# A state-space layer with a small mixture of experts: LayerNorm statistics on ScalarE, the experts' relus on VectorE, a router without its division

## The chip, the cores and the metric

The kernel runs on one core of a Trainium2 chip. The metric is the device time of one execution in microseconds (us). The core has five engines that run side by side, each from its own queue in order: TensorE (PE in the profile, with its weight loads as PEld), VectorE (DVE), ScalarE (ACT), GpSimd (POOL) and SyncE (SP), which only issues DMAs here. A difference of 0.5% (about 10 us) is about what a measurement of this kernel can tell from no change.

## The reference

The input `u` has 4 sequences of 2048 rows of 256 numbers. The layer is

```python
x = x + ssm(layernorm(x), ...)        # selective state space, 512 channels, 16 states each
x = x + moe(layernorm(x), ...)        # 4 experts, the best 2 of them per row

# ssm, per step of the sequence
dA = exp(dt_t[..., None] * A);  dB = dt_t[..., None] * Bt[:, None, :]
h = h * dA + x_t[..., None] * dB
y_t = einsum('bdn,bn->bd', h, Ct)

# moe
scores = softmax(x @ Wg.T + bg);  topv, topi = top_k(scores, 2)
w = sum(one_hot(topi) * topv)
h = relu((x @ Wi.T)[:, None, :] + lora)      # lora: a rank-4 term of each expert
out = einsum('bse,bsed->bsd', w, h @ Wo.T)
```

All numbers are fp32. The hidden width of the experts is 1024. The base product `x @ Wi.T` and the output product with `Wo` are shared by the experts; only the rank-4 term differs.

## The kernel before

The rows are cut into 16 chunks of 512 (`NCHUNK`), four per sequence. Sizes that matter: `P` = 128 partitions, `NJ` = 4 blocks of 128 rows in a chunk, `DM` = 256, `E` = 4 experts.

**The loop.** Each chunk has 64 "states": four blocks of 128 channels times 16 states. Line 996 loops over all 1024 states. For a state, `decay` (line 858) lets ScalarE compute `dA = exp(a * delta)` for 512 time steps, `enter` (line 863) lets GpSimd compute the inputs `dBx` of two states at once, `scan` (line 875) lets VectorE run the recurrence, `read` (line 888) multiplies the result by `C` (on VectorE, tile `hC`; for 5 states in 16 on GpSimd, tile `hP`), and `sum_y` (line 902) lets PE add it up, transposed, in PSUM (tile `y`). `keep` copies the last column to `carry` on ScalarE. ScalarE writes the `dA` of a state two states ahead of the scan (`AHEAD_A`), and GpSimd's `dBx` is four ahead (`AHEAD_B`).

**Work around the loop.** For each chunk there is a front (LayerNorm of the next chunk, `layernorm_T` with the names `ua`, `xn_a`; the input products `pin`; `delta` with a softplus; `xdt`; a gate `g` with a silu), and, after the chunk's last scan, a tail (`po`, the output product) and the experts (`ffn`, line 587): LayerNorm (`xn_f`, `x2T`), router (`plg`), and then eight pieces k = 0..7 (4 blocks of 128 rows times the 2 halves of the hidden width). For each k, `p_low` and `p_base` make the pre-activation `pz` in one PSUM bank, a relu makes `h`, `p_hT` transposes it (`phT`), `a_hT` copies it to `hT`, and `p_down` makes the output `pf`, which `add` adds to `u`.

**Statistics.** `stats` (line 334) runs `bn_stats` and `bn_aggr` on VectorE for each of the 4 blocks; `rstd` (line 341) is four small GpSimd instructions; `norm` applies scale and bias on ScalarE.

**Two experts in one bank.** A row's second expert (slot 1) is computed first: its rank-4 term and the base are added up in the bank and ScalarE takes `relu(topv1 * z)`. Then PE adds the difference of the two rank-4 terms to the same bank and ScalarE takes `relu(topv0 * z)` (`a_relu`, line 734, two calls for each k). `p_hT` adds the two by transposing both into one PSUM bank. In the last chunk alone (`late`) it goes another way: `ratio` (line 721) divides the second weight by the first, ScalarE takes the first relu with that ratio, `d_relu` (line 729) on VectorE takes `max(z, 0) + h`, only one tile is transposed, and `add` multiplies by the first weight.

**The order.** The order of instructions on each engine is decided by a planner when the program is built (`Pacer`, line 45). It carries a planned clock for each engine, and each piece of work is a `Step` with an engine, a cost in us and the steps that it comes after. The loop's own steps are written in order; `fill` (line 107) places waiting steps between them as long as they are planned to start and end close to VectorE's planned time. A VectorE step is placed only if what it waits for on other engines is planned to end 0.7 us earlier (`LATENCY` plus `MARGIN`). `begin` (line 926) hands the threads of steps to the planner; the next chunk's first four `stats` steps are made ready by the softplus of the chunk before:

```python
stats = norms[c + 2][:NJ]
stats[0].after = [loaded, st[c + 1]["soft"]]
```

Once the last scan is written, `drain` writes what is left. PSUM has three banks (`BANKS`) for all work around the loop.

Of the kernel before, what the change touches and what calls it, by code (L numbers as in the profile page):

```python
# [8 lines left out]
F32 = mybir.dt.float32  # L9
AF = mybir.ActivationFunctionType  # L10
ALU = mybir.AluOpType
# [161 lines left out]
def ssm_moe_layer_kernel(  # L173
# [40 lines left out]
    NCHUNK = B * CPB  # L214
    SHARED = (0, 3, 6, 9, 12)
# [114 lines left out]
    def layernorm_T(src, dst, name, then=None):  # L330
# [3 lines left out]
        def stats(j):  # L334
            if j == 0:
                q["mv"] = small.tile([P, NJ, 2], F32, tag=f"mv{name[0]}", name=f"mv_{name}")
            x = small.tile([P, 6], F32, tag="st", name=f"st_{name}_{j}")
            dve.bn_stats(x, src()[:, j, :])
            dve.bn_aggr(q["mv"][:, j, :], x)

        def rstd():

            ve = small.tile([P, NJ], F32, tag="ve", name=f"ve_{name}")
            q["rstd"] = small.tile([P, NJ], F32, tag="rstd", name=f"rstd_{name}")
            q["nmr"] = small.tile([P, NJ], F32, tag="nmr", name=f"nmr_{name}")
            pool.tensor_scalar_add(ve, q["mv"][:, :, 1], EPS)
            pool.tensor_tensor(q["rstd"], ve, mhalf, ALU.pow)
            pool.tensor_tensor(ve, q["mv"][:, :, 0], q["rstd"], ALU.mult)
            pool.tensor_scalar_mul(q["nmr"], ve, -1.0)

        def norm(j):
            q["xn", j] = work.tile([P, DM], F32, tag=f"xn{j}", name=f"xn_{name}_{j}", bufs=1)
            act.activation(
                q["xn", j], src()[:, j, :], AF.Identity,
# [15 lines left out]
        steps = [Step("dve", 0.54, lambda j=j: stats(j)) for j in range(NJ)]  # L370
        steps += [Step("pool", 1.95, rstd)]
# [215 lines left out]
    def ffn(c):  # L587
# [31 lines left out]
        def exp_():  # L619
            for j in range(NJ):  # L620
                act.activation(room(1)[:, j, :], room(0)[:, j, :], AF.Exp, bias=q["red"][:, j : j + 1])

        def softmax():
            sm = small.tile([P, NJ], F32, tag="sm", name=f"sm_{c}")
            dve.tensor_reduce(sm, room(1), AX.X, ALU.add)
            dve.reciprocal(sm, sm)
            p_ = q["p"] = small.tile([P, NJ, E], F32, tag="p_", name=f"p_{c}")
            dve.tensor_tensor(p_, room(1), sm[:, :, None].to_broadcast([P, NJ, E]), ALU.mult)
            dve.tensor_copy(room(2), p_)
# [4 lines left out]
            p_j = room(2)[:, :, None, :].to_broadcast([P, NJ, E, E])  # L634
            p_i = p_[:, :, :, None].to_broadcast([P, NJ, E, E])
            dve.tensor_tensor(eq, p_j, p_i, ALU.is_equal)
            dve.tensor_tensor(gt, p_j, p_i, ALU.is_gt)
            dve.tensor_tensor(eq, eq, lower[:, None, :, :].to_broadcast([P, NJ, E, E]), ALU.mult)
            dve.tensor_tensor(eq, eq, gt, ALU.add)
            dve.tensor_reduce(room(1), eq, AX.X, ALU.add)  # L640

            m = q["m"] = small.tile([P, TOPK, NJ, E], F32, tag="m", name=f"m_{c}")
            for k in range(TOPK):
                dve.tensor_scalar(m[:, k], room(1), float(k), None, ALU.is_equal)
# [12 lines left out]
        def top():  # L657

            m = q["m"]
            mp = small.tile([P, TOPK, NJ, E], F32, tag="mp", name=f"mp_{c}")  # L660
            pool.tensor_tensor(mp, m, q["p"][:, None, :, :].to_broadcast([P, TOPK, NJ, E]), ALU.mult)
            s["topv"] = fold(mp, (P, TOPK, NJ), "topv").rearrange("p k j o -> p k (j o)")
# [58 lines left out]
        def ratio():  # L721

            s["top0"] = small.tile([P, NJ], F32, tag="top0", name=f"top0_{c}", bufs=1)
            dve.tensor_copy(s["top0"], s["topv"][:, 0, :])
            r = small.tile([P, NJ], F32, tag="sm", name=f"r_{c}")
            dve.reciprocal(r, s["top0"])
            dve.tensor_tensor(s["topv"][:, 1, :], s["topv"][:, 1, :], r, ALU.mult)

        def d_relu(k):

            q["h", k, 0] = q["h", k, 1]
            dve.scalar_tensor_tensor(q["h", k, 1], q["z", k], 0.0, q["h", k, 1], ALU.max, ALU.add)

        def a_relu(k, slot):

            h = q["h", k, slot] = scanp.tile([P, HF], F32, tag="hC", name=f"h{slot}_{c}_{k}", bufs=4) if late else work.tile([P, HF], F32, tag=f"h{slot}", name=f"h{slot}_{c}_{k}")
            act.activation(h, q["z", k], AF.Relu, scale=s["topv"][:, slot, k // 2 : k // 2 + 1])

        def p_hT(k):

            pm = q["hT", k] = mm_tile(f"phT_{c}_{k}")
            for slot in (1,) if late else (1, 0):
                for b in range(HF // P):
                    pe.matmul(
                        pm[:, b * P : (b + 1) * P], lhsT=q["h", k, slot][:, b * P : (b + 1) * P], rhs=ident,
                        is_transpose=True, start=(slot == 1 and b == 0), stop=late or slot == 0,
                        skip_group_check=True,
                    )

        def a_hT(k):  # L750
            j, half = divmod(k, 2)
            if half == 0:
                q["h", j] = wide.tile([P, NF, P], F32, tag="hT", name=f"hT_{c}_{j}", bufs=2)
            act.copy(
                q["h", j][:, half * (NF // 2) : (half + 1) * (NF // 2), :],
# [3 lines left out]
        def p_down(j, half):  # L759
            if not half:  # L760
                q["f", j] = mm_tile(f"pf_{c}_{j}")
            for f in range(half * (NF // 2), (half + 1) * (NF // 2)):
                pe.matmul(
                    q["f", j][:, :DM], lhsT=q["h", j][:, f, :], rhs=wo_sb[:, f, :], start=(f == 0), stop=(f == NF - 1)
                )

        def add(j):
            if late:
                dve.scalar_tensor_tensor(
# [340 lines left out]
```

## Time and profile before

| | |
|---|---|
| time, three runs | 2033.55, 2043.07, 2044.17 us; median 2043.07 |
| profiled execution | span 2037.5 us from first to last instruction; its own time is not listed apart from the three |
| busy in the span | PE 1820.4 us (89%), DVE 1818.6 (89%), POOL 1779.0 (87%), ACT 1424.0 (70%) |
| first scan, last scan's end | 31.0 us, 1924.9 us |
| after the last scan | to 2037.5 us: the experts of the last two chunks |
| mean granted TensorE clock | 0.950 |

The median lies 5.6 us above the profiled span. Busy times count overlapping instructions of one engine once, so they are less than count times mean. In the profile's rows a group is: line, engine, operation, output<-inputs, shapes, count, then busy us, mean ns of one, then the engine's idle time just before them and what ended it. Nearly all instructions have line 30, a helper, so they are told apart by their tiles. `ACT_TABLE_LOAD` is ScalarE loading the tables of another function; there are 64, two around each softplus and two around each silu.

### The profile page before, as it was taken

Reading aid. Unit: us, or ns where it says so; the run is one execution under the profiler, and the core shown is the slowest. Engines: PE = TensorE matmul, PEld = TensorE weight load, DVE = VectorE, ACT = ScalarE, POOL = GpSimd, SP = SyncE. Lnnn points to the kernel's source line nnn. Section 1 sums busy time; section 2 is a strip of 40 time slices with the busy share of each in tenths; the row PEclk is TensorE's granted clock in tenths of the full one; section 3 lists DMA queues with packets and bytes.
Section 4 is the critical chain, followed back from the end, with each engine's and each line's share of the span. In section 5 each row is a group of like instructions: output and inputs, shape, how many; then the busy total and the mean of one; then the engine's idle time right before and its main releaser. Section 6 shows DMA issues by size and latency. Waiting matters only on the chain.

```text
span 2037.5 us, 28634 instructions
## 1 busy us (share of the span) xinstructions
PE 1820.4 (89%) x9472; PEld 1251.9 (61%) x9472; DVE 1818.6 (89%) x2370; ACT 1424.0 (70%) x2890; POOL 1779.0 (87%) x1148
## 2 busy tenths in 40 slices
PE   7577798797998998999889899999999898998899
PEld 4445476566666675766557575666756566575655
DVE  3999999899999999999989899899999999899811
ACT  4677777676777768777686777677696877766432
POOL 4999999898999998999998998899999998999600
PEclk8688899798999999999999999999999999998999
DMA  7444445344445453454535344354544544454200
GB/s 237 151 163 157 143 148 171 130 157 164 158 145 166 149 171 137 159 176 144 182 129 175 133 166 149 126 168 141 178 152 160 164 147 158 135 175 145 74 0 21
DMA packets 106132, 300.70 MB, mean 148 GB/s; under 512 B 12864, under 2 KB 39104, under 8 KB 105984
## 3 DMA queue, kind: packets, MB, share of 16 engines
q1 hardware_dynamic: 105984, 298.88, 43.9%
q8 instruction: 74, 1.21, 0.2%
q14 instruction: 74, 0.61, 0.1%
HBM read 289.41 MB, written 9.44 MB: 147 GB/s over the span
## 4 chain that ended last, share of the span: by engine, by line
PE 29%; DVE 14%; ACT 10%; issue 4%; POOL 1%; DMA 0%; DVEq 0%; POOLq 0%; ACTq 0%
PE pz L30 10%; PE y L30 6%; DVE dA L30 6%; PE pf L30 5%; ACT dA L30 4%; PE pin L30 3%; DVE hS L30 3%; DVE hC L30 3%; PE phT L30 2%; ACT L30 1%; ACT delta L30 1%; ACT g L30 1%; PE po L30 1%; DVE u L30 1%; POOL dBx L30 1%
## 5 line engine op out<-in xcount | busy, mean ns | idle before, releaser
L30 POOL TENSOR_TENSOR dBx<-xdt,B 128x1024 f32<-128x1024 f32 x512 | 1205.7, 2363 | 60.4 <-DVE dA L30 20.6
L30 ACT ACTIVATE dA<-delta,a_sb 128x512 f32<-128x512 f32 x1024 | 708.5, 694 | 144.7 <-DVE hC L30 89.6
L30 DVE TENSOR_TENSOR_SCAN dA<-dA,carry,dBx 128x512 f32<-128x512 f32 x528 | 661.1, 1277 | 38.7 <-ACT dA L30 28.2
L30 DVE TENSOR_TENSOR hC<-dA,C 128x512 f32<-128x512 f32 x704 | 470.8, 669 | 0.0
L30 PE MATMUL y<-ident,hC 128*128 128x128 f32 x2816 | 431.8, 284 | 24.4 <-DVE hC L30 24.3
L30 POOL TENSOR_TENSOR hP<-hS,C 128x512 f32<-128x512 f32 x320 | 408.1, 1275 | 2.8 <-PE y L30 2.4
L30 PEld LDWEIGHTS y<-ident,hC 128*128 128x128 f32 x2816 | 344.2, 147 | 105.3 <-DVE hC L30 39.7
L30 DVE TENSOR_TENSOR_SCAN hS<-dA,carry,dBx 128x512 f32<-128x512 f32 x240 | 305.2, 1272 | 22.3 <-ACT dA L30 17.3
L30 PE MATMUL pin<-xnT,w_in_sb 128*128 128x512 f32 x512 | 252.0, 620 | 23.2 <-ACT dbc L30 5.3
L30 PE MATMUL pz<-wi_sb,x2T 128*128 128x512 f32 x512 | 266.1, 645 | 0.0
L30 PEld LDWEIGHTS y<-ident,hP 128*128 128x128 f32 x1280 | 159.7, 147 | 163.9 <-issue 79.8
L30 ACT COPY carry<-dA 128x1 f32<-128x1 f32 x528 | 82.9, 157 | 241.5 <-DVE hC L30 240.3
L30 PE MATMUL y<-ident,hP 128*128 128x128 f32 x1280 | 205.9, 286 | 50.4 <-POOL hP L30 50.2
L30 PE MATMUL pf<-wo_sb,hT 128*128 128x256 f32 x1024 | 238.6, 381 | 6.8 <-ACT hT L30 3.9
L30 DVE TENSOR_TENSOR_SCAN dA<-dA,dBx 128x512 f32<-128x512 f32 x176 | 209.6, 1219 | 14.8 <-ACT dA L30 11.8
L30 ACT ACTIVATE h<-pz,topv 128x512 f32<-128x512 f32 x248 | 167.1, 679 | 77.4 <-PE pz L30 76.6
L30 PEld LDWEIGHTS pf<-wo_sb,hT 128*128 128x128 f32 x1024 | 187.3, 190 | 35.1 <-ACT hT L30 5.2
L30 PE MATMUL pz<-bm_sb,lowT 16*128 16x512 f32 x512 | 167.7, 650 | 23.8 <-ACT delta L30 6.9
L30 PEld LDWEIGHTS pz<-wi_sb,x2T 128*128 128x128 f32 x512 | 93.0, 202 | 121.0 <-issue 121.0
L30 PEld LDWEIGHTS pin<-xnT,w_in_sb 128*128 128x128 f32 x512 | 92.7, 198 | 116.5 <-issue 80.1
L30 PE MATMUL phT<-ident,h 128*128 128x128 f32 x992 | 132.2, 275 | 6.0 <-ACT delta L30 3.1
L30 PEld LDWEIGHTS phT<-ident,h 128*128 128x128 f32 x992 | 114.6, 142 | 31.3 <-issue 17.4
(99 smaller groups left out, 1786.6 us busy)
## 6 DMA issues: line engine op xcount, KB each, us to landing
B<-bc SPq DMA_DIRECT2D x256, 512.0 KB, 3.7
C<-bc SPq DMA_DIRECT2D x256, 512.0 KB, 3.8
ua<-in_u_dram SPq DMA_DIRECT2D x16, 512.0 KB, 5.3
u<-in_u_dram SPq DMA_DIRECT2D x16, 512.0 KB, 5.4
out_dram<-u SPq DMA_DIRECT2D x16, 512.0 KB, 4.8
w_in_sb<-in_w_inT_dram SPq DMA_DIRECT2D x2, 512.0 KB, 4.7
wi_sb<-in_wiT_dram SPq DMA_DIRECT2D x1, 1024.0 KB, 7.2
wo_sb<-in_woT_dram SPq DMA_DIRECT2D x1, 1024.0 KB, 10.6
```

Of the source, the lines that this page charges most:

```text
L30: return self._tc.keep_in_program_order(f(*args, **kwargs))
```

## The change

- `stats` is gone. `mean(j)` is a ScalarE `Copy` with scale -1/256 whose accumulator gives minus the mean; `spread(j)` is a ScalarE `Square` with that as bias, whose accumulator gives the sum of squared differences. Both write a scrap tile `junk`. There are eight ScalarE steps (`NS = 2 * NJ`) where four VectorE steps stood. `rstd` has three GpSimd instructions in place of four.
- The router keeps the exponentials `e` unnormalised. The accumulator of `exp_` gives their sum, whose reciprocal is the first expert's weight `top0` (the largest exponential is 1); the second's, divided by it, is `rho`. The sum, the product and a copy on VectorE are gone, a small copy on ScalarE is new, and the GpSimd instructions of `top` are smaller.
- The way of the last chunk is taken in every chunk: ScalarE takes one relu for each k, with `rho`; VectorE's `d_relu` adds the other; PE transposes one tile; `add` is a multiply and add.

```diff
@@ layernorm_T
-        def stats(j):
...
-            dve.bn_stats(x, src()[:, j, :])
-            dve.bn_aggr(q["mv"][:, j, :], x)
+        def mean(j):
...
+            act.activation(
+                junk, src()[:, j, :], AF.Copy, scale=-1.0 / DM, accum_out=q["nm"][:, j : j + 1]
+            )
+        def spread(j):
...
+            act.activation(
+                junk, src()[:, j, :], AF.Square, bias=q["nm"][:, j : j + 1], accum_out=q["sq"][:, j : j + 1]
+            )
...
-            pool.tensor_scalar_add(ve, q["mv"][:, :, 1], EPS)
+            pool.tensor_scalar(ve, q["sq"], 1.0 / DM, EPS, ALU.mult, ALU.add)
             pool.tensor_tensor(q["rstd"], ve, mhalf, ALU.pow)
-            pool.tensor_tensor(ve, q["mv"][:, :, 0], q["rstd"], ALU.mult)
-            pool.tensor_scalar_mul(q["nmr"], ve, -1.0)
+            pool.tensor_tensor(q["nmr"], q["nm"], q["rstd"], ALU.mult)
...
-        steps = [Step("dve", 0.54, lambda j=j: stats(j)) for j in range(NJ)]
-        steps += [Step("pool", 1.95, rstd)]
+        steps = [Step("act", 0.4, lambda j=j: mean(j)) for j in range(NJ)]
+        steps += [Step("act", 0.45, lambda j=j: spread(j)) for j in range(NJ)]
+        steps += [Step("pool", 1.7, rstd)]
@@ ffn: router
             for j in range(NJ):
-                act.activation(room(1)[:, j, :], room(0)[:, j, :], AF.Exp, bias=q["red"][:, j : j + 1])
+                act.activation(
+                    room(1)[:, j, :], room(0)[:, j, :], AF.Exp, bias=q["red"][:, j : j + 1],
+                    accum_out=q["sm"][:, j : j + 1],
+                )
+            act.copy(q["e"], room(1))
         def softmax():
-            dve.tensor_reduce(sm, room(1), AX.X, ALU.add)
-            dve.reciprocal(sm, sm)
-            dve.tensor_tensor(p_, room(1), sm[:, :, None].to_broadcast([P, NJ, E]), ALU.mult)
-            dve.tensor_copy(room(2), p_)
+            dve.reciprocal(s["top0"], q["sm"])
...
@@ ffn: relus
-        def ratio():
...
-        def a_relu(k, slot):
+        def a_relu(k):
...
-            act.activation(h, q["z", k], AF.Relu, scale=s["topv"][:, slot, k // 2 : k // 2 + 1])
+            act.activation(h, q["z", k], AF.Relu, scale=s["rho"][:, k // 2 : k // 2 + 1])
...
         def p_hT(k):
-            for slot in (1,) if late else (1, 0):
-                for b in range(HF // P):
-                    pe.matmul(
-                        pm[:, b * P : (b + 1) * P], lhsT=q["h", k, slot][:, b * P : (b + 1) * P], rhs=ident,
-                        is_transpose=True, start=(slot == 1 and b == 0), stop=late or slot == 0,
-                        skip_group_check=True,
-                    )
+            for b in range(HF // P):
+                pe.transpose(pm[:, b * P : (b + 1) * P], q["h", k][:, b * P : (b + 1) * P], ident)
         def add(j):
-            if late:
...
-            else:
-                dve.tensor_tensor(s["u"][:, j, :], q["f", j][:, :DM], s["u"][:, j, :], ALU.add)
+            dve.scalar_tensor_tensor(
+                s["u"][:, j, :], q["f", j][:, :DM], s["top0"][:, j : j + 1], s["u"][:, j, :], ALU.mult, ALU.add
+            )
@@ ffn: steps
-            Step("act", 0.85, exp_),
-            Step("dve", 2.25, softmax, gives=1),
-            Step("pool", 1.1, top),
+            Step("act", 0.95, exp_),
+            Step("dve", 1.75, softmax, gives=1),
+            Step("pool", 0.85, top),
...
-                if late:
-                    hs.append(Step("dve", 0.6, lambda k=k: d_relu(k - SK), after=[low, z1s[k - SK]]))
-                else:
-                    hs.append(Step("act", 0.57, lambda k=k: a_relu(k - 1, 0), after=[low], gives=1))
+                hs.append(Step("dve", 0.6, lambda k=k: d_relu(k - SK), after=[low, z1s[k - SK]], gives=int(not late)))
...
-                steps.append(Step("pe", 0.44 if late else 0.88, lambda k=k: p_hT(k - SK), after=[hs[-1]], takes=1))
+                steps.append(Step("pe", 0.44, lambda k=k: p_hT(k - SK), after=[hs[-1]], takes=1))
@@ begin
-                stats = norms[c + 2][:NJ]
+                stats = norms[c + 2][:NS]
                 stats[0].after = [loaded, st[c + 1]["soft"]]
```

## The prediction

> **What bounds the kernel now.** I read the busy shares first, then the same by chunk, then VectorE's waits between 40 and 1900 us, and last the timelines around the longest of those waits.
>
> ```profile
> PE 1820.4 (89%) x9472; PEld 1251.9 (61%) x9472; DVE 1818.6 (89%) x2370; ACT 1424.0 (70%) x2890; POOL 1779.0 (87%) x1148
> ```
>
> Three engines look full. The table by chunk separates them (us, busy PE, PEld, DVE, ACT, POOL with counts, clock, DMA share, GB/s):
>
> ```profile
> 31.00:143.70 112.70, 78.74 (x340) 51.28 (x340) 103.31 (x126) 75.08 (x165) 110.14 (x65) 0.80 0.53 176
> 855.90:971.60 115.70, 111.93 (x615) 78.69 (x613) 113.54 (x149) 84.61 (x136) 111.77 (x73) 1.00 0.49 160
> 1926.00:2037.50 111.50, 105.07 (x431) 63.99 (x429) 16.95 (x45) 30.90 (x54) 3.10 (x10) 0.97 0.03 10
> ```
>
> The first is chunk 0 with no experts yet, the second chunk 7, the third everything after the last scan. In the loop's chunks with experts VectorE is busy 108 to 115 us of 114 to 126: the loop advances as fast as VectorE's queue does. After the loop PE alone is full. So a microsecond in the loop is lost when VectorE works longer or stands still:
>
> ```profile
> DVE dA L30 <- ACT dA L30: 40.0, 77, 3.7
> DVE hS L30 <- ACT dA L30: 21.2, 26, 2.9
> DVE g L30 <- PE py L30: 0.7, 1, 0.7
> DVE u L30 <- PE po L30: 0.5, 1, 0.5
> ```
>
> (us in total, times, longest.) All its waits there are 82.1 us, 61.2 of them for ScalarE's `dA`. Its waits for PE are 1.2 us in about 150 additions of PE's results: PE is busy, but VectorE does not feel it. The long waits sit at ScalarE's table switches. A switch is load, silu or softplus, load: 1.28 + 1.91 + 1.28 = 4.5 us in which no `dA` is written. Here is one where VectorE has little else to do, and then one where it has `bn_stats`:
>
> ```profile
> 490.65 0.17 DVE L30 TENSOR_REDUCE red<-plg 128x4 f32<-128x16 f32 x1
> 490.74 1.28 DVE L30 TENSOR_TENSOR_SCAN dA<-dA,carry,dBx 128x512 f32<-128x512 f32 x1
> 491.93 0.67 DVE L30 TENSOR_TENSOR hC<-dA,C 128x512 f32<-128x512 f32 x1
> 494.82 1.28 DVE L30 TENSOR_TENSOR_SCAN hS<-dA,carry,dBx 128x512 f32<-128x512 f32 x1 [2.22 <-ACT dA L30]
> ```
>
> ```profile
> 1483.79 0.42 DVE L30 BATCH_NORM_STATS2 st_f<-u 128x6 f32<-128x256 f32 x1
> 1484.24 0.18 DVE L30 BATCH_NORM_AGGREGATE mv_f<-st_f 128x2 f32<-128x6 f32 x1
> 1484.34 0.39 DVE L30 BATCH_NORM_STATS2 st_f<-u 128x6 f32<-128x256 f32 x1
> 1484.76 0.18 DVE L30 BATCH_NORM_AGGREGATE mv_f<-st_f 128x2 f32<-128x6 f32 x1
> 1485.05 2.35 DVE L30 TENSOR_TENSOR_SCAN dA<-dA,dBx 128x512 f32<-128x512 f32 x2
> ```
>
> The silus are at 490.81 and 1481.06. In the first the scan waits 2.22 us for `dA`; in the second, where the statistics fill the time until `dA` is back, no wait at all is printed. I did this for all 31 switches after the first: small VectorE work standing beside the last three scans before the switch is the cover, VectorE's idle time from the load to 7 us after the function's start is the stall. Five have a cover of 1.2 us or less (at 55, 356, 491, 1054 and 1760 us) and stall 2.25, 2.88, 2.22, 2.12 and 3.66, mean 2.63. The other 26 have 1.9 us or more, mostly the four `bn` pairs, and stall 0.62 on average. Together that is 29.3 us. A straight line through the 31 gives 2.23 less 0.54 per us of cover.
>
> **VectorE's work.** A `bn` pair advances the queue by 0.535 us (eight entries in sequence, start to start). Each of 15 chunks loses eight: -4.28. The relu's row (`h<-pz,h`, 692 ns) is 23 ns longer than `hC<-dA,C` (669 ns), which advances the queue by 0.59; so 0.61, eight times: +4.88. Four `pf` additions go from 405 to 484 ns: +0.32. The router's stretch takes 2.31 us and loses three instructions, start to start 0.18, 0.21 and 0.22: -0.61. Sum +0.3 a chunk, **+5 us** in all. VectorE is given no relief.
>
> **What waits anew.** A relu waits for PE's second rank-4 term and for ScalarE's relu; behind it stand the next scan and, behind that, GpSimd's `hP` and ScalarE's next `dA`. The planner's rule is that of the 150 additions that waited 1.2 us, so 120 relus cost 1 us; from above 0.5 us each would be 60, as in the stage after the loop, where they waited 20.7 us eight times, but there PE sets the pace. I take 1 us, within the 5.
>
> **The lost cover.** The built order of the changed kernel tells what stands at the switches: 25 of 31 have a cover of 1.2 us or less, among them all but one of the silus. The relus do not replace the statistics there: they are spread over the eight pieces. And the next chunk's eight ScalarE statistics start directly behind the softplus, where ScalarE is already behind. Priced by the two groups, 25 at 2.63 and 6 at 0.62 make 69.5, 40 more than 29.3; by the line, with a mean cover of 0.83, 1.78 each make 55, 26 more. Not below zero, since work that fills a gap cannot lengthen it. I take **+30 us**.
>
> **ScalarE's work.** 120 relus go, at 0.60 each (679 ns less 80 of overlap): -72. 256 statistics come. None is in the trace; the nearest rows are `xn` (256 wide, four in 2.06 us, 0.51 each, two pointer operands) and the router's exponentials (4 wide, four in 1.05, 0.26 each). From below 0.26; from above 0.51 + 0.26 for an accumulator that has to be read out, 0.77. I take 0.45, nearest to `xn` with fewer operands: +115. The exponentials' 64 accumulators at half of 0.26 and 16 copies at 0.2 (the row of `low`) add 11. Net +54, from -5 to +136, on an engine that is 70% busy: mostly beside other work. The waits outside the switches (82.1 - 29.3 = 53 us) can go either way: half the relus and half the waits for `pz` go, the statistics come. I take **-5**, from -26 (half of it) to +38 (the extra 0.32 us of each of 16 statistics in 15 chunks, 77 us, half of it felt by VectorE).
>
> The Trainium skill ("ScalarE: Activation LUTs", What ACT_TABLE_LOAD costs) gives an ACTIVATE 186 ns plus 0.833 ns per element, 93 more for a pointer operand, and 93 of overlap. The estimate by it is 0.31 for a mean and 0.40 for a spread, 91 us in all, with no word on an accumulator's price.
>
> **PE and GpSimd.** 120 times eight transposes become four, 1.04 becoming 0.60 us: -53 us. In the loop VectorE waits 1.2 us for PE, so I give nothing; a PE that fills less may be clocked lower. The rows: chunk 0, PE busy 79 of 113 us, clock 0.80; chunk 7, 112 of 116, clock 1.00. The Trainium skill ("TensorE: Matmul & The Clock Gate", Part 1) halves the clock after an idle window of about 3.4 us, a rule against this change. If it took the clock from 1.00 to 0.96, PE would need about 4 us a chunk more and the saving of 3.5 would be gone; if it does not bind, the saving stays, off the path either way. GpSimd loses 0.30 a `rstd` 32 times and little in `top`: -11 us, not on the path.
>
> **Before and after the loop.** At the start four `bn` pairs (2.2 us) become eight ScalarE instructions (3.6; 2.1 to 6.2), `rstd` is 0.3 shorter, and the first transposes start at 12.56, 1.4 us after `xn` ends: 0, up to +3. After the loop PE is the path. Before, `y` of the last two states stood behind `plT`, which waited 3.4 us for the router's mask; in the new order the router is some three states earlier: -2.8. Chunk 14's transposes: 8 x 0.44 = -3.5. Against it, the last LayerNorm's eight ScalarE statistics stand between `po` and `pt_f`: the addition, 3.6, 1.7 for `rstd` and 2.1 for `xn` are 8.1 (0.7 for the addition), with PE work of 6.7 beside it (`pf` 3.45, rank-4 terms 1.05, base 1.75, transposes 0.44): +1.4. Sum **-5**, from -8 to +2.
>
> **The sum.** 5 + 30 - 5 - 5 + 0 = +25 us. On the span 2037.5 that is 2062.5; the median of the times lies 5.6 above the span, so **2068 us**.
>
> **The rivals.** (1) Faster: PE and ScalarE set the pace of the relu stage. For it: the chain of waits puts 29% of the span on PE, and in the loop ScalarE stood idle for `pz` 28.8 us. Against: VectorE's 1.2 us. Then half of the 53 us outside the switches goes, -26, the stage after the loop gives -5, VectorE's work is +5, and the relus cover most switches, +5: 2043 - 21 = 2022 us. It decides once the waits outside the switches shrink by more than those at the switches grow plus 5. (2) The accumulators are dear: 0.77 us a statistic, queued behind each softplus, +38 in place of -5: 2111 us. (3) The cover is made good: gates and relus fill the switches, +3 in place of +30: 2041 us, no change.
>
> **How the numbers follow.** Main forecast 0.53, rival 1 0.14, rival 2 0.14, rival 3 0.19. The main case's own range is 2046 to 2098 us: from +26 at the switches, -20 outside and 5 - 8 elsewhere to +40, +8 and 5 + 2. The whole range, 2030 to 2100, takes in rival 3, the upper half of rival 1 and the lower part of rival 2. Slower by over 0.5% (10 us, about what a measurement can tell from no change) has the main case and rival 2, 0.67; no change has rival 3 but for 0.01, 0.18; faster has rival 1 and that 0.01, 0.15.
>
> **What would show it.** Right: VectorE's waits for `dA` grow from 61 to about 85 us or more, with over 2 us at most silus; DVE busy within 10 us of 1819; PE near 1765; ACT near 1480. The statistics' own rows settle 0.45. Wrong: waits for `dA` at or below 61, or relus that wait for `pz` by tens of us in the loop, or DVE busy well off.

## The result, and the profile after

The changed kernel takes 2124.24 us (median of 4 runs, 2122.62 to 2125.67); the kernel before, on the same chip, 2041.42 (2033.55 to 2044.17). The ratio is 1.0405, 95% interval 1.0375 to 1.0435: 83 us slower, where 25 were forecast. The profiled execution took 2124.59 us, its span is 2122.8. Its busy shares:

```profile
PE 1851.6 (87%) x8992; PEld 1251.2 (59%) x8992; DVE 1824.0 (86%) x2183; ACT 1482.5 (70%) x3362; POOL 1772.1 (83%) x1116
```

VectorE works 5 us more, as the sum had it. PE has 480 matmuls fewer and is yet busy 31 us longer. The same three stretches as before (chunk 0, chunk 7, after the last scan; us, busy PE, PEld, DVE, ACT, POOL with counts, clock, DMA share, GB/s):

```profile
31.50:159.90 128.40, 87.59 (x335) 54.52 (x334) 99.72 (x109) 82.02 (x192) 113.80 (x65) 0.73 0.45 155
896.20:1017.40 121.20, 107.37 (x556) 73.16 (x556) 113.88 (x137) 87.77 (x164) 109.91 (x65) 0.95 0.49 166
2010.60:2122.80 112.20, 105.26 (x404) 63.15 (x403) 20.78 (x41) 30.05 (x67) 2.75 (x9) 0.94 0.03 10
```

Nothing was lost after the loop (112.6 us before, 112.2 now). Chunk 0 went from 112.7 to 128.4 us, chunk 7 from 115.7 to 121.2 with the same VectorE work. VectorE's waits between 40 and 1900 us (us in total, times, longest):

```profile
DVE dA L30 <- ACT dA L30: 61.1, 79, 3.6
DVE hS L30 <- ACT dA L30: 28.4, 24, 4.7
DVE dA L30 <- ACT carry L30: 16.8, 6, 7.9
DVE hS L30 <- ACT carry L30: 15.7, 10, 2.8
DVE dA L30 <- POOL xdt L30: 11.0, 2, 10.3
...
DVE u L30 <- PE pf L30: 6.8, 8, 2.2
DVE h L30 <- PE pz L30: 4.4, 5, 2.6
```

All waits there are 169 us, before 82. ScalarE's `dA` stands for 28 us of the growth, `carry` (ScalarE's copy in front of the next `dA`) for 22, and one wait of 10.3 us in chunk 0, for the next chunk's front, is new. VectorE's waits for PE grew too, from 1.2 us to 18.2. The two `carry` groups before the change were

```profile
DVE hS L30 <- ACT carry L30: 7.2, 8, 2.7
DVE dA L30 <- ACT carry L30: 3.5, 7, 1.3
```

One softplus in the changed kernel, first VectorE's and then ScalarE's timeline (start, us, engine; idle time before in brackets):

```profile
594.04 0.67 DVE L30 TENSOR_TENSOR hC<-dA,C 128x512 f32<-128x512 f32 x1
597.47 1.22 DVE L30 TENSOR_TENSOR_SCAN hS<-dA,dBx 128x512 f32<-128x512 f32 x1 [2.76 <-ACT carry L30]
...
601.32 1.23 DVE L30 TENSOR_TENSOR_SCAN dA<-dA,dBx 128x512 f32<-128x512 f32 x1 [0.51 <-issue]
```

```profile
593.37 1.92 ACT L30 ACTIVATE delta<-delta 128x2048 f32<-128x2048 f32 x1
...
598.12 0.40 ACT L30 ACTIVATE jm_a<-ua 128x256 f32<-128x256 f32 x1
598.43 0.19 ACT L30 ACTIVATION_READ_ACCUMULATOR jm_a<-ua 128x1 f32 x1
598.64 0.42 ACT L30 ACTIVATE jm_a<-ua 128x256 f32<-128x256 f32 x1
598.97 0.19 ACT L30 ACTIVATION_READ_ACCUMULATOR jm_a<-ua 128x1 f32 x1
...
603.76 0.56 ACT L30 COPY hT<-phT 128x512 f32<-128x512 f32 x1
```

VectorE has nothing between 594.7 and 597.5; ScalarE, late already, then spends most of 598.1 to 603.8 on eight statistics. Each is an `ACTIVATE` and a separate read of the accumulator: 0.54 us from start to start for a mean, 0.61 for a spread.

**One account for all kernels.** From VectorE's timeline I take its idle time between the first and the last scan, and split it: at the 31 switches (1.3 us before to 7 us after the start of each silu and softplus) and outside them. "Loop" is first to last scan start, "after" the rest of the span. (Counted so, the switches of the kernel before hold 33.8 us, where the prediction's count gave 29.3.) All in us but the ratio (to the kernel before on the same chip) and the clock. The median is of all runs of a kernel, the columns from "loop" on are of the one profiled execution.

| kernel | median | ratio (95%) | loop | idle at switches | idle outside | after | clock |
|---|---|---|---|---|---|---|---|
| before | 2041.4 | 1 | 1892.6 | 33.8 | 62.8 | 113.9 | 0.950 |
| changed | 2124.2 | 1.0405 (1.0375-1.0435) | 1977.8 | 68.8 | 108.2 | 113.4 | 0.908 |
| stats_only | 2192.2 | 1.0754 (1.0738-1.0770) | 1984.5 | 107.8 | 136.8 | 172.2 | 0.904 |
| relu_only | 2137.0 | 1.0482 (1.0466-1.0498) | 1986.0 | 42.9 | 87.6 | 116.9 | 0.914 |
| router_only | 2034.5 | 0.9977 (0.9963-0.9991) | 1884.9 | 34.4 | 61.1 | 117.4 | 0.945 |
| front_bn | 2142.9 | 1.0524 (1.0492-1.0556) | 1960.5 | 58.0 | 82.5 | 143.5 | 0.908 |
| light_stats | 2093.7 | 1.0249 (1.0233-1.0265) | 1947.7 | 68.3 | 84.5 | 110.9 | 0.916 |
| turn_twice | 2135.8 | 1.0450 (1.0430-1.0469) | 1986.5 | 69.3 | 114.2 | 116.0 | 0.919 |
| planned_costs | 2115.2 | 1.0354 (1.0319-1.0390) | 1940.6 | 78.5 | 72.3 | 132.1 | 0.921 |
| measured_costs | 2135.8 | 1.0468 (1.0431-1.0505) | 1981.5 | 82.2 | 98.6 | 118.8 | 0.900 |
| noswitch_before | 2008.1 | 0.9849 (0.9803-0.9896) | 1858.1 | 7.9 | 58.3 | 113.9 | 0.952 |
| noswitch_after | 2069.8 | 1.0147 (1.0112-1.0182) | 1921.0 | 18.4 | 103.7 | 115.8 | 0.921 |
| relu_light | 2119.2 | 1.0390 (1.0353-1.0428) | 1969.2 | 47.5 | 120.2 | 115.8 | 0.913 |
| relu_warm | 2127.2 | 1.0435 (1.0400-1.0470) | 1979.6 | 42.8 | 82.2 | 114.2 | 0.929 |
| light_warm | 2101.4 | 1.0299 (1.0274-1.0324) | 1962.6 | 47.5 | 114.0 | 112.7 | 0.937 |
| relu_early | 2135.9 | 1.0461 (1.0439-1.0483) | 1987.3 | 42.7 | 88.3 | 112.3 | 0.914 |
| relu_costs_13 | 2132.6 | 1.0461 (1.0431-1.0490) | 1984.3 | 46.3 | 81.7 | 114.3 | 0.909 |
| relu_costs | 2100.9 | 1.0291 (1.0271-1.0311) | 1952.5 | 46.5 | 51.0 | 114.4 | 0.913 |
| relu_costs_19 | 2101.0 | 1.0308 (1.0283-1.0333) | 1959.3 | 44.4 | 61.3 | 108.8 | 0.914 |
| mix_two | 2032.6 | 0.9947 (0.9925-0.9970) | 1882.9 | 34.5 | 58.6 | 116.8 | 0.939 |

So the 85 us by which the loop grew are 5 of VectorE's work, 35 at the switches and 45 outside them. The prediction had 5, 30 and -5.

Two finer cuts of the same count. Of the 35 us at the switches, 21 came at the softplus (14.3 to 35.5 us in total) and 14 at the silus (19.4 to 33.2). Of the 45 outside them, 15.5 stand in chunk 0 (5.6 to 21.1).

### The profile page after: what moved, and what is told of

Read it like the earlier page. It is cut to its first block, busy times and chain, and to the rows that moved or that the text cites. A ratio compares the mean times of both kernels' runs of the same rounds, so it can differ in the third digit from the quotient of the medians.

```text
span 2122.8 us, 27884 instructions
## 1 busy us (share of the span) xinstructions
PE 1851.6 (87%) x8992; PEld 1251.2 (59%) x8992; DVE 1824.0 (86%) x2183; ACT 1482.5 (70%) x3362; POOL 1772.1 (83%) x1116
## 5 line engine op out<-in xcount | busy, mean ns | idle before, releaser
L30 PE MATMUL y<-ident,hC 128*128 128x128 f32 x2816 | 457.8, 296 | 46.8 <-DVE hC L30 46.4
L30 PEld LDWEIGHTS y<-ident,hC 128*128 128x128 f32 x2816 | 362.5, 153 | 150.3 <-DVE hC L30 71.2
L30 PE MATMUL y<-ident,hP 128*128 128x128 f32 x1280 | 218.7, 298 | 51.3 <-POOL hP L30 51.2
L30 PEld LDWEIGHTS y<-ident,hP 128*128 128x128 f32 x1280 | 166.4, 153 | 161.6 <-POOL hP L30 68.2
L30 PE MATMUL pf<-wo_sb,hT 128*128 128x256 f32 x1024 | 245.0, 386 | 10.4 <-ACT hT L30 9.5
L30 PE MATMUL pz<-bm_sb,lowT 16*128 16x512 f32 x512 | 183.3, 671 | 28.3 <-ACT carry L30 8.4
L30 ACT ACTIVATE h<-pz,rho 128x512 f32<-128x512 f32 x128 | 86.8, 678 | 82.2 <-PE pz L30 81.9
L30 PE MATMUL po<-w_out_sb,g 128*128 128x256 f32 x512 | 125.0, 389 | 2.8 <-DVE u L30 2.4
L30 DVE SCALAR_TENSOR_TENSOR h<-pz,h 128x512 f32<-128x512 f32 x128 | 86.8, 678 | 41.5 <-PE pz L30 41.3
```

What stands on the lines that cost most here:

```text
L30: return self._tc.keep_in_program_order(f(*args, **kwargs))
```

## The experiments

Three theories. **Cover**: without `bn` pairs VectorE stands at the table switches. **Statistics**: the accumulators cost more than planned, and `dA` and the next front come late behind them. **PE**: an emptier PE is clocked lower, and everything that waits for it is late.

### The change in parts

**stats_only**: the kernel before with the change's `mean`, `spread` and `rstd`, and nothing else (its scrap tile is in bf16, and the planner's prices are 0.42 and 0.47 in place of 0.40 and 0.45).

```diff
-            dve.bn_stats(x, src()[:, j, :])
-            dve.bn_aggr(q["mv"][:, j, :], x)
+            junk = work.tile([P, DM], mybir.dt.bfloat16, tag="junk", ...)
+            act.activation(junk, src()[:, j, :], AF.Copy, scale=-1.0 / DM, accum_out=q["nm"][:, j : j + 1])
...
+            act.activation(junk, src()[:, j, :], AF.Square, bias=..., accum_out=q["sq"][:, j : j + 1])
```

> Only the statistics go to ScalarE (scrap tile in bf16); relus and router stay as before. Common to all: VectorE loses 8 bn pairs a chunk, 15 x 4.28 = -64 us. Cover theory: the switches cost about 35 us more, as in the changed kernel, and the front of chunk 1 is late by some 15: -64 + 50, about 2028 us. Statistics theory (0.54 and 0.61 us each, not the planned 0.40 and 0.45, in front of dA everywhere): another +30 or more outside the switches, about 2058 us or above, with waits for dA of 90 us or more. PE theory: PE has its old work, so the clock stays near 0.95 and VectorE's waits for PE stay under 5 us; 2028 us.

Measured: 2192.2 us, 152 above the kernel before, far beyond the figure of any theory. VectorE is relieved of 56 us and stands 148 us more in the loop, half at the switches and half outside, and 58 us are added after the loop, where PE has 656 matmuls to do in place of 432: work that found no place in the loop. Its longest groups of waits (40 to 1980 us):

```profile
DVE dA L30 <- ACT dA L30: 54.7, 93, 4.6
DVE u L30 <- PE po L30: 43.6, 9, 9.4
DVE dA L30 <- ACT carry L30: 38.4, 14, 8.3
DVE dA L30 <- POOL xdt L30: 37.1, 4, 12.0
```

The last line is the front of the next chunk coming late, four times. ScalarE with both relus and the statistics (busy 1549.6 us, before 1424.0, so 0.49 us a statistic) no longer keeps the loop supplied. Alone, the part of the change that lightens VectorE is the dearer one.

**relu_only**: the changed kernel with the `bn` pairs (and the `rstd`) of the kernel before.

```diff
-        steps = [Step("act", 0.4, lambda j=j: mean(j)) for j in range(NJ)]
-        steps += [Step("act", 0.45, lambda j=j: spread(j)) for j in range(NJ)]
+        steps = [Step("dve", 0.54, lambda j=j: stats(j)) for j in range(NJ)]
```

> The new relus and the new router, but bn statistics on VectorE. Common to all: VectorE gains 15 x 4.59 = +69 us, PE loses 53 and ScalarE 72. Cover theory: switches cost as before, 34 us, waits outside as before: about 2110 us. Statistics theory: the same or up to 10 less, since ScalarE is relieved: 2100. PE theory: the granted clock falls to about 0.91 and VectorE's waits for PE (1.2 us before) grow to about 19 as in the changed kernel: about 2130 us.

Measured: 2137.0. Busy VectorE is 63 us longer, near the +69. The switches cost 43 us in place of the changed kernel's 69, as cover theory has it: the softplus, which have their `bn` pairs again, stall 9 us in place of 35. The silus still stall 34: in this order only 3 of 16 have `bn` pairs beside them (11 before the change), and these three stall 0.1 to 0.3 us each. But 25 us of the waits outside the switches are there without a single ScalarE statistic, which none of the theories has. (The PE theory named its clock, 0.914, and its 2130 came nearest, but VectorE's waits for PE are 9 us and not 19.) +152 and +97 do not add up to +83: each part takes work from the engine that the other one loads.

**router_only**: the kernel before with the new router; both relus on ScalarE.

```diff
-            act.activation(h, q["z", k], AF.Relu, scale=s["topv"][:, slot, k // 2 : k // 2 + 1])
+            act.activation(h, q["z", k], AF.Relu, scale=s["rho"][:, k // 2 : k // 2 + 1] if slot else 1.0)
```

> The new router alone: both relus stay on ScalarE, the second expert's scaled by rho, the first's by 1, and the addition multiplies by top0. VectorE: -0.61 + 0.32 a chunk, -4 us. All theories: 2041 - 4, about 2037 us, from 2027 to 2047; above 2050 the router's place in the order matters more than its work.

Measured: 2034.5, ratio 0.9977 (0.9963 to 0.9991). As worked out. The interval leaves out 1, but the gain is 0.2%, less than the 0.5% that a measurement of this kernel can tell from no change: by itself this part does no harm, and its gain is at the edge of what can be seen.

**front_bn**: the changed kernel, the fronts' statistics back on VectorE, the experts' not.

```diff
+        if on_dve(name):      # name[0] == "a"
+            steps = [Step("dve", 0.54, lambda j=j: stats(j)) for j in range(NJ)]
```

> The changed kernel, but the four statistics of each front's LayerNorm (the ones that stand at the softplus) are bn pairs on VectorE again; those of the experts' LayerNorm stay on ScalarE. Common to all against the changed kernel's 2124: VectorE +60 x 0.535 = +32. Cover theory: the stalls at the 15 softplus fall from 35 to about 14 us and the front of chunk 1 is on time (-15): 2124 + 32 - 36 = 2120 us. Statistics theory: besides, half of the extra 45 us outside the switches goes: about 2100 us. PE theory: clock and waits for PE stay: 2120 us or more.

Measured: 2142.9, 19 above the changed kernel. In the loop it went as the cover theory says: the 15 softplus stall 17 us in place of 35, and the first chunk's waits of 7.9 and 10.3 us are gone, so chunk 0 is as short as before the change. Outside the switches there are 26 us less, 15.5 of them in chunk 0; of the statistics theory's further 22 that leaves 10. The silus stall 7 us more, and the loop is 17 us shorter in spite of 29 us more VectorE work. But the other order leaves 534 matmuls for after the last scan (404 in the changed kernel) and that stage is 30 us longer. A gain in the loop can be given back there.

### Which cost makes the waits

**light_stats**: the changed kernel in the same order, each ScalarE statistic on one column and without its accumulator.

```diff
-            act.activation(junk, src()[:, j, :], AF.Copy, scale=-1.0 / DM, accum_out=q["nm"][:, j : j + 1])
+            act.activation(q["nm"][:, j : j + 1], src()[:, j, :1], AF.Copy, scale=-1.0 / DM)
...
-            act.activation(junk, src()[:, j, :], AF.Square, bias=..., accum_out=q["sq"][:, j : j + 1])
+            act.activation(q["sq"][:, j : j + 1], src()[:, j, :1], AF.Square, bias=...)
```

> The changed kernel with the same order, but each of the 256 ScalarE statistics reads and writes one column, without accumulator: about 0.22 us in place of 0.54 (mean) and 0.61 (spread), 90 us less on ScalarE. It leaves out the statistics themselves. Statistics theory: what they cost by their length goes, a good half of the extra 45 us of waits outside the switches and some at the softplus they stand behind: about 2090 us. Cover theory: VectorE has as little to do at the switches as before: 2115 to 2124 us. PE theory: PE's work and clock stay: 2124 us.

Measured: 2093.7, as the statistics theory said. ScalarE is busy 81 us less; outside the switches 24 us of waits go, at the switches 0.5 of 69. So the stalls at the switches do not come from how long the statistics are, and about half of the growth outside does. Chunk 0 takes 122.6 us, between 112.7 and 128.4, and its two long waits, 7.9 and 10.2 us, stay (40 to 1900 us):

```profile
DVE dA L30 <- ACT dA L30: 56.8, 59, 4.5
DVE hS L30 <- ACT dA L30: 22.0, 21, 2.9
DVE hS L30 <- ACT carry L30: 14.7, 9, 2.8
DVE dA L30 <- ACT carry L30: 13.9, 5, 7.9
DVE dA L30 <- POOL xdt L30: 10.2, 1, 10.2
```

**noswitch_before** and **noswitch_after**: the same edit to each kernel, so that ScalarE never changes its tables. The softplus and silu are left out.

```diff
-            act.activation(s["delta"], s["delta"], AF.Softplus)
+            act.activation(s["delta"], s["delta"], AF.Relu)
...
-            act.activation(s["g"], s["g"], AF.Silu)
+            act.activation(s["g"], s["g"], AF.Relu)
```

> The kernel before with Relu in place of each softplus and silu, so that ScalarE never changes its tables (the gate and delta are not the reference's). The stall at the 31 switches, 34 us, falls to a few: all theories about 2010 us.

> The changed kernel with Relu in place of each softplus and silu, no table switches. Cover theory: its 69 us of stall at the switches fall to a few too, about 2060 us, and the distance to the same edit of the kernel before is 83 - 35 = about 48 us. Statistics theory, if the stalls at the switches were really the eight statistics queued behind each softplus: the distance stays at 75 us or more, 2085 us.

Measured: 2008.1 and 2069.8. The distance between the kernels is 61 us (by the two ratios, 0.0298 of 2038) in place of 83, between cover's 48 and the other's 75. Without switches the same stretches still hold 18.4 us in the changed kernel and 7.9 before, so of the 35 us about 24 need the switch, and about 10 stand there without it.

**planned_costs** and **measured_costs**: the changed kernel, prices alone.

```diff
-        steps = [Step("act", 0.4, lambda j=j: mean(j)) for j in range(NJ)]
-        steps += [Step("act", 0.45, lambda j=j: spread(j)) for j in range(NJ)]
+        steps = [Step("act", 0.54, lambda j=j: mean(j)) for j in range(NJ)]
+        steps += [Step("act", 0.61, lambda j=j: spread(j)) for j in range(NJ)]
@@ in measured_costs besides
-            Step("act", 0.95, exp_),
+            Step("act", 1.6, exp_),
```

> The changed kernel, but the planner is told what the statistics took in the trace, 0.54 and 0.61 us in place of 0.40 and 0.45. Statistics theory, in the form that the planner's belief misplaces what follows them: dA and the front come on time, 20 to 30 us less, about 2100 us. Cover theory and PE theory: 2124 us, give or take 10 for another order.

> As planned_costs, and the planner is told too that the four exponentials with accumulator and the copy take 1.6 us (they took 1.72 start to end) in place of 0.95. Planner's-price theory: VectorE's waits outside the switches, 72 us in planned_costs and 63 before the change, fall by some 10 more, and the loop to about 1930 us. If the rest is the relus' own: loop 1940 us as in planned_costs. The stage after the loop moves with the order in either case, 113 to 135 us: 2080 to 2115 us.

Measured: 2115.2 and 2135.8. With the statistics' price right, 36 of the 45 us outside the switches are gone and the loop is 37 us shorter, though 10 come back at the switches; 19 are lost after the loop. That leaves 18 of gain in this execution and 9 between the medians, whose intervals overlap. With the exponentials' price too, the loop is as long as the changed kernel's again. Truer prices shift the waits, and in this kernel they do not reliably remove them.

**turn_twice**: same order, PE filled as before the change.

```diff
-            for b in range(HF // P):
-                pe.transpose(pm[:, b * P : (b + 1) * P], q["h", k][:, b * P : (b + 1) * P], ident)
+            for _ in range(1 if late else 2):
+                for b in range(HF // P):
+                    pe.transpose(pm[:, b * P : (b + 1) * P], q["h", k][:, b * P : (b + 1) * P], ident)
```

> The changed kernel with the same order, but PE transposes each relu tile twice (not in the last chunk), which fills PE as before the change: 480 matmuls more, 53 us at full clock. PE clock theory: the granted clock rises from 0.908 towards 0.95, so PE's other work gets shorter, and the time is 2124 or less, down to 2100 us. If a fuller PE is only a longer PE: clock unchanged, PE later, ScalarE and VectorE wait for it more: 2135 to 2150 us. If PE stands beside the path in the loop: 2124 to 2130 us, 3.5 of it after the loop.

Measured: 2135.8, ratio 1.0450 where the changed kernel has 1.0405 (the intervals overlap). The clock rises only from 0.908 to 0.919, a quarter of the way back to 0.950, and nothing gets faster; in the profiled execution the loop is 9 us longer and the stage after it 3 us. So the saved transposes explain a quarter of the lost clock at most; if anything, saving them was worth some 10 us.

### The waits that came with the relus

**relu_light**: relu_only in the same order, with a short relu.

```diff
-            dve.scalar_tensor_tensor(q["h", k], q["z", k], 0.0, q["h", k], ALU.max, ALU.add)
+            dve.scalar_tensor_tensor(q["h", k][:, :1], q["z", k][:, :1], 0.0, q["h", k][:, :1], ALU.max, ALU.add)
```

> relu_only in the same order, but VectorE's relu works on one column of 512 (the other columns of the second expert's share are left out), about 0.1 us in place of 0.6 in 120 relus of the loop: 60 us less VectorE work. relu_only had 34 us more idle VectorE in the loop than the kernel before. If these come from the relus' place between PE and ScalarE, a dependency that stays: 2137 - 60 = 2077 us and idle 130 us. If from their length: idle falls to about 100, 2045 us. If VectorE's work were not what bounds: above 2100 us.

Measured: 2119.2, worse than any named case but the last. VectorE works 62 us less and stands 37 us more: in this order, something other than the relus' length sets the pace. What is late is ScalarE, and it waits longer for PE's `y` (tiles `yt` and `xd`, 40 to 1980 us): 88 us, in relu_only 77, before the change 52. In relu_only, PE's timeline around a router:

```profile
1006.91 0.66 PE L30 MATMUL y<-ident,hP 128*128 128x128 f32 x4 [2.37 <-POOL hP L30]
1007.47 0.96 PE L30 MATMUL y<-ident,hC 128*128 128x128 f32 x4
1012.53 1.06 PE L30 MATMUL plT<-ident,lowm 128*64 128x128 f32 x4 [4.09 <-POOL lowm L30]
1013.38 1.06 PE L30 MATMUL y<-ident,hC 128*128 128x128 f32 x4
...
1019.63 1.12 PE L30 MATMUL y<-ident,xd 128*128 128x128 f32 x4
...
1023.09 0.60 PE L30 MATMUL y<-ident,hC 128*128 128x128 f32 x4
```

PE stands 4.09 us at `plT` for the router's mask, and after that four transposes take 1.06 us, not 0.60, for ten microseconds. Between 200 and 1900 us there are 12 such stops of over 2.5 us at `plT` in relu_only, 5 in the changed kernel, 1 before. Three runs ask what this costs.

**relu_warm** and **light_warm**: relu_only and relu_light, PE kept at work through the stop.

```diff
             pl = q["pl"] = mm_tile(f"plT_{c}")
+            for n in range(24 if c < NCHUNK - 1 else 0):
+                pe.transpose(pl[:, n % NJ * P : (n % NJ + 1) * P], ident, ident)
```

> relu_only in the same order, with 24 transposes of the identity put in front of the router's transposes plT, into the same bank: some 2.7 us of idle PE at each stop become work. If the slow PE behind the stop is what delays y, dA and the scans: clock up from 0.914, four transposes behind plT at 0.60 again, waits outside the switches down by 15 to 25, about 2115 us. If the stop itself counts and not the clock: 2137 us, or up to 10 more where the mask was in time.

> relu_light (VectorE's relus on one column, the rest left out) with the same 24 transposes in front of plT. If the slow PE behind the stop swallowed VectorE's relief of 57 us: well below relu_light's 2119, about 2085 us, with the waits outside the switches down from 120 to about 90. If not: 2119 us.

Measured: 2127.2 (clock 0.929) and 2101.4 (0.937): 10 and 18 us less than without the extra transposes; the intervals of the first pair touch, those of the second are clear of each other. The slow stretches do cost, but waits outside the switches fall by 5 and 6 us only, so they are not what made most of the 25 us.

**relu_early**: relu_only, GpSimd's part of the router without the comparisons (the choice of experts is left out).

```diff
-            pool.tensor_tensor(me, m[:, 1], q["e"], ALU.mult)
+            pool.tensor_tensor(me, q["e"], q["e"], ALU.mult)
...
-                    q["m"][:, k, :, :, None].to_broadcast([P, NJ, E, LR]),
+                    q["e"][:, :, :, None].to_broadcast([P, NJ, E, LR]),
```

> relu_only in the same order, but GpSimd's part of the router (the second weight and the mask) is computed from the exponentials alone, so it does not wait for VectorE's comparisons (the choice of experts is left out). The stop at plT, 3.6 us, shrinks by some 2 us. If the stop or the clock behind it makes the waits: 2110 to 2120 us. If neither: 2137 us.

Measured: 2135.9. PE's wait at `plT` falls from 46.6 to 20.5 us in total, and the time stays. The length of these stops is not the cause.

**relu_costs**, **relu_costs_13**, **relu_costs_19**: relu_only with another price of the exponentials. (The four exponentials with their accumulator reads and the copy took 1.72 us, from 1011.89 to 1013.61 in the changed kernel; the four were 1.05 in the kernel before.)

```diff
-            Step("act", 0.95, exp_),
+            Step("act", 1.6, exp_),      # 1.3 and 1.9 in the other two
```

> relu_only, but the planner is told 1.6 us in place of 0.95 for the four exponentials and their copy. Price theory: the mask is planned later, the stop at plT falls from 3.6 us to about 1, and the time to about 2115 us. Otherwise 2137, give or take 12 for another order.

> relu_only with 1.3 us as the planner's price of the four exponentials and the copy (0.95 in relu_only: 2137 us; 1.6 in relu_costs: 2101; 1.72 measured). Price theory: between the two, 2105 to 2125 us, with idle VectorE in the loop near 110. Luck of the order: anything from 2095 to 2140, not in line with the price.

> relu_only with 1.9 us as that price, a little above the measured 1.72. Price theory: as relu_costs, 2095 to 2107 us, idle near 98. Luck of the order: back up to 2115 to 2140.

Measured: 0.95 gives 2137.0 us, 1.3 gives 2132.6, 1.6 gives 2100.9 and 1.9 gives 2101.0. The waits of relu_costs, between 40 and 1980 us:

```profile
DVE dA L30 <- ACT dA L30: 38.9, 47, 3.1
DVE dA L30 <- ACT carry L30: 13.8, 13, 2.2
DVE dA L30 <- issue: 8.1, 10, 2.3
DVE hS L30 <- ACT dA L30: 7.0, 13, 1.1
```

Idle VectorE in the loop is 97.5 us, before the change 96.6: the relus' 25 us outside the switches are all gone, and what is left, +60 us, is VectorE's own work (+62.5 busy). The clock, 0.913, is that of relu_only, so the mean clock is not what made the difference. But 1.3 missed the 2105 to 2125 of the price theory: the four orders show a step between 1.3 and 1.6, and no more.

Where the price puts the router can be read from the traces. Count the scans that have begun, from the start of the exponentials' own chunk (64 are its end), when the exponentials start. In relu_only they start at 60 to 73 in chunks 4 to 13, in eight of these ten chunks at 60 to 63. In relu_costs all ten start at 68. With 1.3 five start at 68 and five at 59 or 60; with 1.9 nine start at 68; with the three higher prices none of the ten starts between 61 and 67. Two rules of the planner fit this (lines 51, 132, 55 and 140 of the kernel before, and line 998, where `PER // NH` is 32):

```python
LONG = 1.0
if self.quiet and x.engine == "act" and x.cost > self.LONG:
    return False
END = {"pe": 2.2, "act": 1.5, ...}
... (t + x.cost <= v + self.END[x.engine] or t <= v - 0.5)
pacer.quiet = (i + 5) % (PER // NH) < 8
```

A ScalarE step priced above 1.0 us is kept out of eight states round the end of each half chunk, and one priced above 1.5 must moreover start earlier than VectorE's planned time. So a higher price can move the exponentials by these rules alone, whether it is true or not, and 1.3 and 1.6 lie on two sides of the second one. The runs do not separate a truer price from a price that trips a rule. In measured_costs the exponentials of chunks 3 to 13 start at 68 too, and its loop is 41 us longer than that of planned_costs. Shown is that in relu_only about 36 us hang on the order that this price brings; which of its placements does it was not singled out.

### The one-transpose way for two chunks

**mix_two**: the kernel before with the new router, and the one-transpose way for the last two chunks only.

```diff
+        mix = c >= NCHUNK - 2
...
-            for slot in (1,) if late else (1, 0):
+            for slot in (1,) if mix else (1, 0):
...
-                if late:
+                if mix:
                     hs.append(Step("dve", 0.6, lambda k=k: d_relu(k - SK), after=[low, z1s[k - SK]], ...))
```

> The kernel before with the new router, and the last chunk's way (one relu on ScalarE, one on VectorE, four transposes) for the last two chunks in place of one: the change only where PE sets the pace. After the loop PE loses up to 8 x 0.44 = 3.5 us, VectorE gains 0.61 for each of the 8 relus that stands in the loop. Prediction's term for the stage after the loop: 2034.5 - 3.5 = 2031 us; if the pieces stand in the loop, 2034 to 2038 us.

Measured: 2032.6, ratio 0.9947 (0.9925 to 0.9970). Beside router_only's 0.9977 the intervals overlap, and its stage after the loop, 116.8 us, is no shorter than before. With the router both versions come out ahead of the kernel before, by 0.2 and 0.5%, and the one-transpose way adds nothing that can be told from no change.

## Why the prediction was right or wrong, step by step

- **VectorE's work, +5.** Right: 1818.6 to 1824.0 busy.
- **The lost cover, +30.** Right in mechanism and near in size: +35 at the switches, 33.8 to 68.8. Filling the softplus again (relu_only, front_bn) took the stalls there back, shortening the statistics did not, and the silus without `bn` pairs stalled on in relu_only. That the sum came so near is in part luck: without switches about 10 of the 35 stand in the same stretches, which leaves about 25 for this mechanism, just under the term's 26 to 40.
- **Waits outside the switches, -5 (from -26 to +38).** This step failed: +45, above its upper end. The statistics' length made about 24 of it (light_stats). The term's price for one, 0.45, was too low: 0.54 and 0.61 from start to start, since each is followed by an accumulator read of 0.19 us. The prediction had the read only in its upper bound, where it was 0.26. Against this the term set the relief from half of the relus, which did not come: relu_only, without any ScalarE statistic, stands 25 us more outside the switches and not less, and these 25 hang on the planner's order: another price for the router's exponentials took them all away. The prediction took the planner's rule as kept (1 us for the relus) and did not ask what else the new order would move. Direct waits for `pz` were 4.4 us, so that part was near; in relu_only ScalarE waited longer for PE's `y`. In the changed kernel itself the two halves cannot be added up, since every price makes another order: how much of its 45 belongs to the relus stays open.
- **Chunk 0.** Not in the prediction: its front for chunk 1, now eight ScalarE statistics longer, came late, and 15.7 of the 85 us are there; 15.5 us of the 45 are this. With the front's statistics on VectorE (front_bn) the chunk takes 112.7 us again; with short ones on ScalarE (light_stats) 122.6. So about 6 of the 15.7 go with their length and 10 with their place and number.
- **ScalarE, +54.** +58.5, right. By parts, stats_only +126 (115 forecast) and relu_only -61 (-61): an engine total that is right says little about its lateness.
- **PE relief, 0, and the clock.** Wrong for PE, and not nothing for the time: PE's busy time rose by 31 us in place of -53, the clock fell from 0.950 to 0.908, and VectorE's waits for PE rose from 1.2 to 18.2 us. The emptier PE explains a quarter of the lost clock at most (turn_twice). What goes with it is stops: PE gaps of over 2.5 us between 200 and 1900 us were 10 before and 22 after, and filling the stops at `plT` raised the clock from 0.914 to 0.929 (relu_warm) and from 0.913 to 0.937 (light_warm). For the changed kernel this was not tried. The Trainium skill ("TensorE: Matmul & The Clock Gate", Part 1) halves the clock after an idle window of about 3.4 us. Here four transposes take 1.06 us in place of 0.60 after most stops of over 2.5 us. The prediction weighed that rule and put it off the path; light_warm shows 18 us of it on the path of relu_light, and relu_warm 10 on that of relu_only, where the intervals touch.
- **After the loop, -5.** -0.5, inside the bounds of -8 to +2. That this stage can grow by 19, 30 and 58 us when work is left over from the loop (planned_costs, front_bn, stats_only) was not in the sum at all.
- **The rivals.** The dear accumulators (2111) were the right rival in mechanism, not in size: a statistic advanced ScalarE by 0.54 and 0.61 us, not by 0.77, and the statistics' length cost about half of what was missing (light_stats is 31 us faster, the forecast was 56 too low). The faster rival asked for fewer waits outside the switches and the no-change rival for filled switches; +45 and +35 speak against them.

## What to carry to other kernels

Where a planner writes the order, an operation's price in it is part of the change. One price, for four exponentials and a copy, was worth 36 us in relu_only, where VectorE's relus themselves cost 63; the same price made planned_costs some 20 us slower. So look up what each new operation really advances its queue by, its accumulator read included, look in the planner for the thresholds that a price can cross, and then measure: a truer price is not by itself a better order. Moving work off the busiest engine gained nothing here (stats_only), because the engine that feeds it became late: of two engines, count how late the feeder comes, not how full it is. Judge the parts of a change alone as well as together; here the router was the only part that did no harm.

## What the runs showed of the hardware

- An accumulator output costs a separate instruction on ScalarE. In the changed kernel's groups (count, then busy us and mean ns):

```profile
L30 ACT ACTIVATE js_f<-u,nm_f 128x256 f32<-128x256 f32 x64 | 32.3, 504 | 1.0
...
L30 ACT ACTIVATE jm_f<-u 128x256 f32<-128x256 f32 x64 | 26.2, 410 | 1.5 <-DVE u L30 1.1
...
L30 ACT ACTIVATION_READ_ACCUMULATOR jm_f<-u 128x1 f32 x64 | 12.2, 191 | 0.0
```

- PE was slow after stops of well under 3 us too. Over four kernels (before, changed, stats_only, relu_only; between 200 and 1900 us, stops whose next work is a group of four transposes), that group was slow, about 1.1 us for 0.6, after 19 of 106 stops of 1 to 2 us, 16 of 37 of 2 to 3 us, and 45 of 48 longer ones; some of the short ones lie in a slow stretch that had begun earlier. Counting only stops before which the last group of four had still taken 0.7 us or less, it was 2 of 20 at 2 to 2.5 us, 4 of 8 at 2.5 to 3, and 25 of 27 above 3. After a stop of over 2.5 us the first group at 0.7 us or less came 8.9 us later in the changed kernel and 10.6 in relu_only (medians over the 20 and 19 stops with a slow stretch behind them).
